# Layer 3's attention of three images among the last expert tiles, in a four-layer hybrid network

## The chip, the cores and the metric

The kernel runs on one core of a Trainium2 chip, as one launch. The metric is the device time in microseconds, the median of several runs of the whole program; one further execution is recorded by the hardware profiler, and all views below come from that one.

The engines are named as the profile names them: PE is TensorE's matmul, PEld its weight load, DVE is VectorE, ACT is ScalarE, POOL is GpSimd, SP is SyncE. An engine works through its own instructions in order, and semaphores make it wait for others. A name with q behind it (ACTq, SPq, POOLq) is the engine issuing DMAs.

## What is computed

Input `x` is (4, 256, 32, 32): four images (B) of 1024 tokens (L) with 256 channels (D), so 4096 tokens (T). Everything is float32. Four layers follow one another:

- Layer 0: a Mamba-2 block with squeeze-and-excitation. Layer 1: a non-local block of 1x1 convolutions. Neither is touched.
- Layer 2: self-attention, then a mixture of experts. Every token goes to the best two of eight experts (E); an expert is two matrices, 256x1024 and 1024x256, with an exact gelu between.
- Layer 3: a linear attention with batch norm, and then an LSTM of 1024 steps over the tokens.

Cut to what matters here:

```python
# layer 2, feed forward: _ln_t normalises each token over its channels
logits = xf @ Wg + bg
top_w, top_i = top_k(logits, 2); top_w = softmax(top_w)
out = sum over e of  w_dense[:, e] * (gelu(xf @ W1[e] + b1[e]) @ W2[e] + b2[e])
t = t + out
# layer 3, attention, for each image; f = _ln_t(t)
query, key = f @ W_qk[0] + b_qk[0], f @ W_qk[1] + b_qk[1]
sm = softmax(key, axis=tokens)
lam = einsum('bnd,bne->bde', sm, f @ W_v + b_v)
bn = batchnorm(lam)            # over the images and the value channels
t = t + einsum('bnd,bde->bne', query, bn)
# layer 3, feed forward: an LSTM over the tokens, h and c start at 0
i, f, o = sigmoid(x_t U + b + h V);  g = tanh(x_t U_c + b_c + h V_c)
c = h * c + i * g;  h = o * tanh(c)
```

The batch norm of `lam` runs over all four images, so nothing behind it can start before the last image's `lam`. The first three images' `lam` do not need the last image.

## The kernel before

**Experts** (`_layer2_experts`). Tokens are scattered by expert into a DRAM buffer `sorted`, and worked in tiles of 256 rows (TS). There are 36 tiles (NTILE), in an order written out at the head of the function: 17 "first" tiles (NFULL), filled from the routing of images 0 to 2 alone, so that they run while the last image's routing is still worked out beside them (`last_image`, advanced by `next(parts, None)`); then 16 "more" tiles (NMORE), with 3 half tiles of 128 rows (NHALF) spread between them. Three further halves (NREST) stand behind a runtime condition, `tc.If(need > NHALF)`; with this input they are not run, but every engine passes there.

For each tile, `fetched` (two tiles ahead) has POOL gather the expert's weights `w` (128 x 4360 floats, L1249) and the token rows (L1255). `turned` computes where each result goes (`place`, DVE, L1271 or L1273), transposes the rows on PE (`pt`, L1277) and copies them to `uT` (DVE, L1279). `worked` runs the first matrix on PE (`ph`, L1300), gelu on ACT (`hT`, L1292), the second matrix for the two halves of the tile (`po`, L1334), adds the bias and scales on DVE (`y`, L1339 and L1340), and scatters to a DRAM buffer `results` (POOL, L1341). A half tile goes through `raw` instead (L1314 to L1322). `turned` of the next tile is called between the two `po` of a tile; the instruction scheduler then decides each engine's order. `po` has two PSUM banks in the pool `moe_ps2`, `ph` three, `pt` one. A scatter of one tile and the next one are kept in order by `place`, which is written while the scatter before it may still read its other buffer.

**Layer 3's attention** (`_layer3_attention`) starts when the last expert result has landed. Image by image: SP loads the two results of each token (`y_in`, L1486, sixteen loads of 512 KB, three buffers of two); DVE adds them to the rows (L1491) and takes the statistics (L1495, L1496), and a short Newton iteration (`_rsqrt`) gives the scale; ACT normalises (`rows`, L1476); PE transposes (`p_x`, L1442) and DVE copies to `u` (L1446); PE multiplies by the key matrix (L1517), ACT adds the bias (L1522), DVE takes the maximum (L1529), ACT the exponential with its sum (L1532); PE transposes the keys (`p_k`, L1542), DVE copies (`kt`, L1544), PE accumulates `p_u` (L1546); a last product with the value matrix gives `lam` (L1556, L1560). The rows are also transposed to `x_l` (ACT copies, L1445). The queries (L1573) and the batch norm (`bn_stats` L668, L1592) follow the last image.

**The LSTM** (`_layer3_lstm`): a lead-in (folding the queries' matrix into `lam`, L1642, the first norm, L1707 to L1748, and the input products, L1674), and then 1024 steps in which PE, DVE and ACT answer one another. Its weights `b_l`, `w_u`, `w_v` and the four matrices of `w_l3` are loaded on ACT's queue (L1404, L186) as the attention begins.

The order in which the code writes its work out is all that the programmer sets; each engine's final order comes from a list scheduler which goes by modelled costs. Two lines are kept for the tile order:

```python
order.append(("more", i))
order += [("half", h) for h in range(i * NHALF // NMORE, (i + 1) * NHALF // NMORE)]
```

Of the kernel before, what the change touches and what calls it, by code (L numbers as in the profile page):

```python
# [11 lines left out]
F32 = mybir.dt.float32  # L12
# [7 lines left out]
P = 128  # L20
# [32 lines left out]
NTILE = NFULL + NMORE + NHALF  # L53
ROW = D + 2
# [29 lines left out]
def _setup(s):  # L84
# [33 lines left out]

    s.spread = s.const.tile([NBLK, NBLK, P], F32, name="spread")
    nc.vector.tensor_copy(s.spread, _bc(s.ident[:NBLK, :NBLK], 2, P))  # L120
# [69 lines left out]
def _layernorm(s, u):  # L190

    nc = s.nc
    with ExitStack() as ctx:
        pool = ctx.enter_context(s.tc.tile_pool(name="ln", bufs=2))
        ps = ctx.enter_context(s.tc.tile_pool(name="ln_ps", bufs=2, space=PSUM))
        ps1 = ctx.enter_context(s.tc.tile_pool(name="ln_ps1", bufs=1, space=PSUM))
        var = ps1.tile([NBLK, W], F32, name="var")
# [20 lines left out]
        for i in range(NBLK):  # L218
            t = bass.ts(i, W)
            wide = ps.tile([P, W], F32, name="wide")  # L220
            nc.tensor.matmul(wide, s.spread[:, i, :], rstd, start=True, stop=True)
            nc.vector.tensor_mul(u[:, :, t], u[:, :, t], _bc(wide, 1, C))
# [496 lines left out]

def _layer2(s):  # L720

# [3 lines left out]
    with ExitStack() as ctx:  # L725
        m = SimpleNamespace(
            keep=ctx.enter_context(tc.tile_pool(name="moe_keep", bufs=1)),
            one=ctx.enter_context(tc.tile_pool(name="moe_one", bufs=1)),
            pool=ctx.enter_context(tc.tile_pool(name="moe_head", bufs=2)),
# [23 lines left out]
        m.views = dram_disjoint_views(s.sorted, 2 * NT)  # L753
        m.counts = None
        _layer2_attention(s, m)
        _layer2_experts(s, m)


def _layer2_attention(s, m):
    nc, tc = s.nc, s.tc  # L760
    scale = D**-0.5
    with ExitStack() as ctx:
        keep = ctx.enter_context(tc.tile_pool(name="l2_keep", bufs=1))
        u = keep.tile([P, C, T], F32, name="u")
# [98 lines left out]
def _head(s, m, b, psum):  # L863
# [97 lines left out]
    before = m.counts  # L961
# [81 lines left out]
def _table(s, m, name, n, tiles):  # L1043
# [5 lines left out]
    t = lambda shape, x: m.one.tile(shape, F32, name=f"{name}_{x}")  # L1049
# [15 lines left out]
def _pick(s, m, name, mine, values):  # L1065

    nc = s.nc
    n, K = mine.shape[1:]
    w = m.one.tile([P, n, K], F32, name=f"{name}_w")
    nc.vector.tensor_mul(w, mine, _bc(values, 1, n))  # L1070
    of = m.one.tile([P, n], F32, name=f"{name}_of")
    nc.vector.tensor_reduce(of, w, AX.X, ALU.add)
    return of


def _weight_rows(s, m, name, expert):

    nc = s.nc
    n = expert.shape[1]
    row = m.one.tile([P, n], F32, name=f"{name}_row")  # L1080
    nc.vector.tensor_scalar(row, expert, float(E - 1), float(P), ALU.min, ALU.mult)
    rows = m.keep.tile([P, n], U32, name=f"{name}_rows")
    nc.vector.tensor_scalar_add(rows, row, s.token[:, :1])
    return rows


def _count(s, m, name, values, n, size, least):

    nc = s.nc
    edges = m.one.tile([P, n], F32, name=f"{name}_edges")  # L1090
    nc.vector.tensor_scalar(edges, m.marks[:, :n], float(size), float(least), ALU.mult, ALU.add)
    over = m.one.tile([P, E, n], F32, name=f"{name}_over")
    nc.vector.tensor_tensor(over, _bc(values, 2, n), _bc(edges, 1, E), ALU.is_ge)
    held = m.one.tile([P, E], F32, name=f"{name}_count")
# [4 lines left out]
def _taken(s, m, name, n, first, tiles):  # L1099

    nc = s.nc
    taken = m.one.tile(list(tiles.shape), F32, name=f"{name}_taken")
# [5 lines left out]
def _first_tiles(s, m):  # L1108
# [7 lines left out]
    base = m.one.tile([P, E], F32, name="f_base")  # L1116
# [11 lines left out]
def _part_tiles(s, m, name, n, A, tiles, start, ahead):  # L1128
# [9 lines left out]
    if K > E:  # L1138
        over = m.one.tile([P, n], F32, name=f"{name}_over")
        nc.vector.tensor_scalar(over, of, float(E), -float(E), ALU.is_ge, ALU.mult)  # L1140
        nc.vector.tensor_add(of, of, over)
# [3 lines left out]
    base = m.one.tile([P, K], F32, name=f"{name}_base")  # L1145
# [4 lines left out]
    at = m.one.tile([P, n, A], F32, name=f"{name}_at")  # L1150
    nc.vector.tensor_tensor(at, _bc(own, 2, A), _bc(s.token[:, :A], 1, n), ALU.add)
    counts = m.one.tile([P, K], F32, name=f"{name}_counts")
# [4 lines left out]
    valid = m.one.tile([P, n, A], F32, name=f"{name}_valid")  # L1157
# [15 lines left out]
    places = m.one.tile([P, n * A], F32, name=f"{name}_ahead")  # L1173
# [8 lines left out]
def _other_tiles(s, m):  # L1182
# [5 lines left out]
    tiles = m.one.tile([P, 2 * E], F32, name="m_tiles")  # L1188
    start = m.one.tile([P, 2 * E], F32, name="m_start")
    nc.vector.tensor_sub(tiles[:, :E], most, m.taken)  # L1190
    nc.vector.tensor_scalar_mul(start[:, :E], m.taken, float(TS))
    yield
    nc.vector.tensor_scalar_mul(start[:, E:], most, float(TS))
    nc.vector.tensor_tensor(tiles[:, E:], m.counts, start[:, E:], ALU.is_gt)
# [3 lines left out]
    begin = m.one.tile([P, E], F32, name="h_start")  # L1198
    nc.vector.tensor_add(begin, taken[:, :E], taken[:, E:])
# [3 lines left out]
    left = m.one.tile([P, E], F32, name="h_left")  # L1203
# [3 lines left out]
    total = m.one.tile([P, 1], F32, name="h_total")  # L1207
# [7 lines left out]
def _layer2_experts(s, m):  # L1215

    nc, tc = s.nc, s.tc
    results = iter(dram_disjoint_views(s.results, 2 * (NFULL + NMORE) + NHALF + NREST))  # L1220
    order = [("first", i) for i in range(NFULL)]
    for i in range(NMORE):
        order.append(("more", i))
        order += [("half", h) for h in range(i * NHALF // NMORE, (i + 1) * NHALF // NMORE)]
    with ExitStack() as body:
        wp = body.enter_context(tc.tile_pool(name="moe_w", bufs=2))
        hp = body.enter_context(tc.tile_pool(name="moe_h", bufs=2))
        rp = body.enter_context(tc.tile_pool(name="moe_r", bufs=3))
        ps = body.enter_context(tc.tile_pool(name="moe_ps", bufs=3, space=PSUM))
        ps2 = body.enter_context(tc.tile_pool(name="moe_ps2", bufs=2, space=PSUM))  # L1230

        def psum():
            return ps2.tile([P, W], F32, name="p_head")

        def last_image():
            yield from _head(s, m, B - 1, psum)
# [3 lines left out]

        def fetched(j):

            kind, i = order[j]
            if kind != "first":
                for _ in parts:
                    pass
            rows, slots = m.tiles[kind][:2]
            w = (wp if j % 3 else m.w).tile([P, NEXP], F32, name="w")
            nc.gpsimd.indirect_dma_start(  # L1249
                w, None, s.d["w12"], bass.IndirectOffsetOnAxis(rows[:, i : i + 1], 0)  # L1250
            )
            A = slots.shape[2]
            row = m.row.tile([P, 2, ROW], F32, name="row")
            for a in range(A):
                got = nc.gpsimd.indirect_dma_start(  # L1255
                    row[:, a, :], None, s.sorted,
                    bass.IndirectOffsetOnAxis(slots[:, i, a : a + 1], 0),
                )
                if kind == "first":

                    m.full.append(got)
            return w, row[:, :A]

        def turned(j):

            kind, i = order[j]
            row = held[j][1]
            A = row.shape[1]
            place = rp.tile([P, 2], U32, name="place")[:, :A]
            if kind == "first":  # L1270
                nc.vector.tensor_copy(place, row[:, :, D + 1])  # L1271
            else:
                nc.vector.tensor_add(place, row[:, :, D + 1], m.tiles[kind][2][:, i, :])  # L1273
            pt = ps2.tile([P, C, A, P], F32, name="pt", bufs=1)
            for k in range(C):
                for a in range(A):
                    nc.tensor.transpose(pt[:, k, a, :], row[:, a, bass.ts(k, P)], s.ident)  # L1277
            uT = rp.tile([P, C, TS], F32, name="uT")[:, :, : A * P]
            nc.vector.tensor_copy(uT, pt.rearrange("p k a t -> p k (a t)"))  # L1279
            return place, uT  # L1280

        def worked(w, row, place, uT, lead):

            A = row.shape[1]
            w1 = w[:, : C * HID].rearrange("p (k n) -> p k n", k=C)
            w2 = w[:, C * HID : C * HID + NHC * D].rearrange("p (k n) -> p k n", k=NHC)
            b1 = w[:, C * HID + NHC * D :][:, :NHC]
            b2 = w[:, C * HID + NHC * D + NHC :]
            hT = hp.tile([P, NHC, TS], F32, name="hT")

            def gelu(n, ph):
                nc.scalar.activation(  # L1292
                    hT[:, n, : A * P], ph, AF.Gelu, bias=b1[:, n : n + 1]
                )

            if A == 2:
                for n in range(NHC):
                    ph = ps.tile([P, W], F32, name="ph")[:, :TS]
                    for k in range(C):
                        nc.tensor.matmul(  # L1300
                            ph, w1[:, k, bass.ts(n, P)], uT[:, k, :],
                            start=k == 0, stop=k == C - 1,
                        )
                    gelu(n, ph)
                    if n % 2:
                        next(parts, None)
                        next(parts, None)
            else:

                raw = rp.tile([P, HID], F32, name="raw", bufs=2)  # L1310
                for i in range(HID // W):
                    ph = ps.tile([P, W], F32, name="ph")
                    for k in range(C):
                        nc.tensor.matmul(  # L1314
                            ph, uT[:, k, :], w1[:, k, bass.ts(i, W)],
                            start=k == 0, stop=k == C - 1,
                        )
                    nc.vector.tensor_copy(raw[:, bass.ts(i, W)], ph)
                for i in range(HID // W):
                    ph = ps.tile([P, W], F32, name="ph")  # L1320
# [664 lines left out]
```

## Time and profile before

| | |
|---|---|
| median of 3 runs | 3393.04 us (3390.83 to 3394.68) |
| profiled execution, its own time | 3408.06 us |
| its span | 3406.3 us |
| mean granted TensorE clock | 0.973 |
| busy: PE / DVE / ACT / POOL | 3177.1 / 1997.0 / 1233.9 / 378.8 us |
| chain that ended last: PE / DVE / ACT / issue / DMA / POOL | 72 / 14 / 5 / 3 / 2 / 1 % |

By stages of the span, PE's busy time and clock:

| stage | window, us | PE busy, us | clock |
|---|---|---|---|
| layers 0 and 1 and layer 2's attention | 0 to 780 | 675.1 | 0.92 to 0.95 |
| first expert tiles, the last image's routing beside | 780 to 1040 | 240.0 of 260 | 0.96 |
| more expert tiles | 1040 to 1255 | 215.0 of 215 | 1.00 |
| the last expert tiles | 1255 to 1311 | 51.4 of 56 | 1.00 |
| layer 3's attention | 1311 to 1450 | 107.8 of 139 | 0.86 |
| lead-in of the LSTM | 1450 to 1475 | 23.9 of 25 | 0.93 |
| LSTM | 1475 to 3406 | 1863.9 of 1931 | 1.00 |

The windows are cut by hand from the trace. A matmul record of the profile is one pass of PE: a float32 product of this kernel shows two records, a transpose one. "Clock" is the share of full speed that was granted to PE in the window.

### The profile page before, as it was taken

How to read it: one execution, taken by the hardware profiler on the slowest of the kernel's cores; microseconds unless marked ns; L12 is line 12 of the kernel's file. 1: busy time of each engine (PE TensorE's matmuls, PEld its weight loads, DVE VectorE, ACT ScalarE, POOL GpSimd, SP SyncE). 2: the span in 40 equal slices, each digit the busy share in tenths (PEclk: the TensorE clock that was granted, in tenths of full speed). 3: DMA queues.
4: the chain of work that ended last, by engine and by line, in shares of the span. 5: the costliest groups of instructions: out<-in, count | busy, mean ns of one | idle time of the engine just before them, and what ended most of it. 6: DMA issues, size and time to landing. Idle time of an engine off the chain costs nothing.

```text
span 3406.3 us, 146430 instructions
## 1 busy us (share of the span) xinstructions
PE 3177.1 (93%) x65186; PEld 2489.1 (73%) x65186; DVE 1997.0 (59%) x8389; ACT 1233.9 (36%) x5057; POOL 378.8 (11%) x468
## 2 busy tenths in 40 slices
PE   7788899998899996999999999999999999999888
PEld 4465344446788884688888888888888888888776
DVE  5696534452211115557777777776777767776666
ACT  4633222223222222433434334343343343443333
POOL 0083002223433330000000000000000000000000
PEclk9899899999999997999999999999999999999999
DMA  1291001115555654000000000000000000000000
GB/s 69 67 298 34 10 0 38 38 36 203 187 195 206 230 212 148 0 3 5 4 11 4 5 11 4 11 4 4 11 4 5 10 4 5 10 5 4 10 4 10
DMA packets 78058, 180.50 MB, mean 53 GB/s; under 512 B 6256, under 2 KB 63920, under 8 KB 72816
## 3 DMA queue, kind: packets, MB, share of 16 engines
q0 software_dynamic: 14880, 106.99, 8.5%
q1 hardware_dynamic: 60624, 59.12, 5.9%
q8 instruction: 511, 8.37, 1.0%
q10 hardware_dynamic: 1920, 5.00, 0.4%
q14 instruction: 123, 1.01, 0.1%
HBM read 111.26 MB, written 59.84 MB: 50 GB/s over the span
## 4 chain that ended last, share of the span: by engine, by line
PE 72%; DVE 14%; ACT 5%; issue 3%; DMA 2%; POOL 1%; ACTq 0%; DVEq 0%; POOLq 0%
PE p_c L1826 11%; PE p_c L1817 8%; PE ph L1300 6%; PE po L1334 6%; DVE turned L1867 6%; PE p_i L1817 5%; PE p_o L1826 5%; PE p_i L1826 5%; PE p_o L1817 5%; PE beside L1767 4%; PE p_mm L850 3%; PE p_s L814 2%; ACT a_o L1868 2%; DVE x L1880 2%; ACT th L1878 1%
## 5 line engine op out<-in xcount | busy, mean ns | idle before, releaser
L1868 ACT ACTIVATE add<-turned 128x8 f32<-128x8 f32 x1024 | 214.3, 209 | 1011.4 <-DVE turned L1867 1011.4
L1826 PE MATMUL p_c<-w_v,x 128*4 128x64 f32 x16368 | 416.7, 219 | 60.6 <-DVE x L1880 57.9
L1817 PE MATMUL p_c<-xg,shift 128*128 128x64 f32 x2048 | 446.0, 299 | 0.0
L1826 PE MATMUL p_o<-w_v,x 128*4 128x64 f32 x16368 | 417.8, 219 | 0.0
L1826 PE MATMUL p_i<-w_v,x 128*4 128x64 f32 x16368 | 417.4, 219 | 0.0
L1817 PE MATMUL p_i<-xg,shift 128*128 128x64 f32 x2048 | 407.7, 281 | 0.0
L1867 DVE STREAM_TRANSPOSE turned<-p_c 128x64 f32<-128x64 f32 x1024 | 255.7, 250 | 253.9 <-PE p_c L1826 220.0
L1817 PE MATMUL p_o<-xg,shift 128*128 128x64 f32 x2048 | 396.4, 275 | 0.0
L1817 PEld LDWEIGHTS p_c<-xg,shift 128*128 128x128 f32 x2048 | 304.9, 188 | 117.6 <-DVE turned L1867 0.4
L1826 PEld LDWEIGHTS p_c<-w_v,x 128*4 128x4 f32 x16368 | 227.9, 85 | 180.8 <-DVE x L1880 102.0
L1880 DVE TENSOR_TENSOR x<-a_o,th 128x8 f32<-128x8 f32 x1024 | 171.2, 167 | 246.0 <-ACT th L1878 246.0
L1817 PEld LDWEIGHTS p_o<-xg,shift 128*128 128x128 f32 x2048 | 311.4, 192 | 0.0
L1817 PEld LDWEIGHTS p_i<-xg,shift 128*128 128x128 f32 x2048 | 305.1, 188 | 0.0
L1826 PEld LDWEIGHTS p_o<-w_v,x 128*4 128x4 f32 x16368 | 281.9, 87 | 0.8 <-issue 0.5
L1826 PEld LDWEIGHTS p_i<-w_v,x 128*4 128x4 f32 x16368 | 281.6, 87 | 0.3
L1867 DVE STREAM_TRANSPOSE turned<-p_i 128x64 f32<-128x64 f32 x1024 | 271.9, 266 | 0.9 <-PE p_i L1826 0.7
L1292 ACT ACTIVATE hT<-ph,w 128x256 f32<-128x256 f32 (+1 forms) x288 | 131.3, 465 | 355.8 <-PE ph L1300 267.3
L1300 PE MATMUL ph<-uT,w 128*128 128x256 f32 x1056 | 241.6, 386 | 19.6 <-DVE uT L1279 11.3
L1867 DVE STREAM_TRANSPOSE turned<-p_o 128x64 f32<-128x64 f32 x1024 | 255.6, 250 | 0.9 <-PE p_o L1826 0.3
L1334 PE MATMUL po<-w,hT 128*128 128x256 f32 x1104 | 251.1, 380 | 2.7 <-ACT hT L1292 1.5
L1868 ACT ACTIVATE a_o<-turned 128x8 f32<-128x8 f32 x1024 | 213.3, 208 | 95.4 <-DVE cell L1871 4.5
L1300 PEld LDWEIGHTS ph<-uT,w 128*128 128x128 f32 x1056 | 203.2, 194 | 50.2 <-DVE uT L1279 12.1
(499 smaller groups left out, 4395.0 us busy)
## 6 DMA issues: line engine op xcount, KB each, us to landing
sorted<-zeros SPq DMA_DIRECT2D x32, 1032.0 KB
y_in<-results SPq DMA_DIRECT2D x16, 512.0 KB
x<-in_x_dram SPq DMA_DIRECT2D x8, 512.0 KB
tokens<-rows SPq DMA_DIRECT2D x4, 1024.0 KB
x<-tokens SPq DMA_DIRECT2D x8, 512.0 KB
out_dram<-x_l SPq DMA_DIRECT2D x64, 64.0 KB
results<-y,place POOLq DMA_INDIRECT x69
w_l<-in_w_l_dram ACTq DMA_DIRECT2D x1, 1092.0 KB
```

What stands on the lines that cost most here:

```text
L814: nc.tensor.matmul(p_s[:, h, :], q[:, k, q0 : q0 + P], u[:, k, b * L + h * W : b * L + (h + 1) * W], start=k == 0, stop=k == C - 1,)
L850: nc.tensor.matmul(p, v[:, n, bass.ts(c, P)], prT[:, n, :], start=n == 0, stop=n == TPI - 1,)
L1292: nc.scalar.activation(hT[:, n, : A * P], ph, AF.Gelu, bias=b1[:, n : n + 1])
L1300: nc.tensor.matmul(ph, w1[:, k, bass.ts(n, P)], uT[:, k, :], start=k == 0, stop=k == C - 1,)
L1334: nc.tensor.matmul(po, hT[:, n, bass.ts(a, P)], w2[:, n, :], start=n == 0, stop=n == NHC - 1,)
L1767: nc.tensor.matmul(p[bass.ts(i, R), :], rows[:, k, bass.ts(g, R)], w_u[:, k, at : at + GQ // GC], start=k == 0, stop=k == C - 1, tile_posi ...
L1817: nc.tensor.matmul(p[:, :H], shift[:, row * B : row * B + P], xg[n][:, g, bass.ts(i, H)], start=True, stop=t == 0,)
L1826: nc.tensor.matmul(p[R * i : R * i + B, :H], hs[:, t - 1, bass.ts(k, B)], w_v[:, k, i * GQ + g * H : i * GQ + (g + 1) * H], start=False, s ...
L1867: nc.vector.transpose(zt.rearrange("p c w -> p (c w)"), pz[g][:, :H])
L1868: nc.scalar.activation(dst.rearrange("p (c b) -> p c b", c=C), zt[:, :, :B], f)
L1878: nc.scalar.activation(th, cell[:, :, 1], AF.Tanh)
L1880: nc.vector.tensor_mul(h, a_o, th)
```

## The change

- A new tile order. The 17 first tiles, then 14 "more" tiles; then the last five, half, more, half, more, half. The tables are built so that these last five tiles (from tile NLAST = 31 on) hold tokens of the last image only: "more" tiles now come in two kinds, those up to an expert's last row of images 0 to 2 and those after. `_other_tiles` has more operations on its small tables for that.
- So the results of images 0 to 2 have all been scattered when tile 30 ends. `first_images()` is a generator of layer 3's work: image 0's rows to `u`; image 0's keys to `lam` in turn with image 1's rows to `u`; image 1's keys in turn with image 2's rows. It is advanced two steps at each place `beside(n)` of the tiles 31 to 35, and emptied before the `If`.
- Behind the `If`, `_layer3_last_image` does the last image's rows in turn with image 2's keys and the first three images' transposes to `x_l`; then the last image's keys, the queries and the batch norm.
- `y_in` loads are single (512 KB) with two buffers; a load is issued after the add two before it.
- The expert stage is two functions, `_first_experts` (17 tiles) and `_last_experts` (19), with pools of their own; at the change of pools the buffers' last users are waited for. In the second one `po` has one PSUM bank, `pt` takes turns with layer 3's transposes and products in two banks; `hT` has one buffer, `place` and `uT` two. Two more banks are layer 3's `p_u`.
- `u`, `lam` and `q` live in a new pool over both layers; `spread` goes from the constants to the norm that uses it; `x` by channel is written over the input's copy, and the LSTM's hidden states have a tile of their own. The LSTM's weights (`b_l`, `w_u`, `w_v`, `wq`) are loaded, on ACT's queue still, where `_layer3_lstm` begins.

The core of the diff:

```diff
+        m.order = [("first", i) for i in range(NFULL)]
+        m.order += [("more", i) for i in range(NLAST - NFULL)]
+        for i in range(NHALF):
+            m.order.append(("half", i))
+            if NLAST - NFULL + i < NMORE:
+                m.order.append(("more", NLAST - NFULL + i))
...
+def _last_experts(s, m):
...
+        l3 = SimpleNamespace(
+            pool=ctx.enter_context(tc.tile_pool(name="l3", bufs=2)),
+            y=ctx.enter_context(tc.tile_pool(name="l3_y", bufs=2)),
+            ps=ctx.enter_context(tc.tile_pool(name="l3_ps", bufs=2, space=PSUM)),
+            pu=ctx.enter_context(tc.tile_pool(name="l3_pu", bufs=1, space=PSUM)),
...
+        def first_images():
+            yield from _rows_to_u(s, l3, 0)
+            for b in range(B - 2):
+                yield from _in_turn(_keys(s, l3, b, nc.vector), _rows_to_u(s, l3, b + 1))
...
+            m.rp = body.enter_context(tc.tile_pool(name="moe_r", bufs=2))
+            m.ps = body.enter_context(tc.tile_pool(name="moe_ps", bufs=3, space=PSUM))
+            m.po = body.enter_context(tc.tile_pool(name="moe_po", bufs=1, space=PSUM))
+            m.hT = m.rp.tile([P, NHC, TS], F32, name="hT", bufs=1)
+            m.bank = lambda name: l3.bank()
...
+                def beside(n):
+                    if j >= NLAST:
+                        for _ in range(2):
+                            next(parts, None)
...
+                done = _worked(s, m, j, *ahead.pop(), lead, beside)
...
+            for _ in parts:
+                pass
...
+            with tc.If(need > NHALF):
...
+        _layer3_last_image(s, l3)
...
+def _rows_to_u(s, l3, b, split=False):
...
+    load()
+    load()
+    yield
+    for i, (g, k) in enumerate(todo):
+        xr = s.xr[:, bass.ts(b * G + g, TPB), :]
+        nc.vector.tensor_add(xr, xr, ys[i])
+        if len(ys) < len(todo):
+            load()
+        yield
...
+        first = chain(_keys(s, l3, last - 1, nc.scalar), *(by_channel(b) for b in range(last)))
+        for _ in _in_turn(_rows_to_u(s, l3, last, split=True), first):
+            pass
+        for _ in _in_turn(_keys(s, l3, last, nc.vector), by_channel(last)):
+            pass
+        for _ in queries():
+            pass
...
+        bias, fold, mask, shift = _lstm_constants(s, keep)
+        w_u = _weights(s, keep, "w_u")
+        w_v = _weights(s, keep, "w_v")
+        wq = keep.tile([P, C, D], F32, name="wq")
+        nc.scalar.dma_start(wq, s.d["w_l3"][:, :D].rearrange("(k p) n -> p k n", p=P))
```

## The prediction

> **What bounds the kernel now.** I read the windows view first, over the end of the expert stage and the attention of layer 3 (columns: window, its length, busy us and instruction count of each engine, granted TensorE clock, DMA share, GB/s):
>
> ```profile
> 1242.00:1256.00 14.00, 14.00 (x69) 12.32 (x68) 1.88 (x7) 3.79 (x8) 4.87 (x5) 1.00 0.57 208
> 1311.00:1326.00 15.00, 1.28 (x6) 0.87 (x6) 9.41 (x32) 1.93 (x4) 0.00 (x0) 0.52 0.88 309
> 1326.00:1347.00 21.00, 15.97 (x38) 6.76 (x36) 15.40 (x36) 7.36 (x13) 0.00 (x0) 0.69 0.58 184
> 1347.00:1380.00 33.00, 27.30 (x103) 17.86 (x104) 28.63 (x97) 10.91 (x21) 0.00 (x0) 0.84 0.25 80
> 1410.00:1446.00 36.00, 32.84 (x145) 22.67 (x144) 13.97 (x31) 8.42 (x14) 0.00 (x0) 1.00 0.00 0
> ```
>
> The experts are bound by PE: 14.00 of 14 us. Then PE does almost nothing for 15 us while layer 3 loads the expert results, and for 54 us more it is busy, but at a granted clock of 0.69 and 0.84. The chain of waits shows a full expert tile on its own, and the hand-over (start, us, what):
>
> ```profile
> 1241.58 6.91 PE ph L1300 x32
> 1248.49 3.45 PE po L1334 x16
> 1251.94 0.44 PE pt L1277 x4
> 1252.38 3.46 PE po L1334 x16
> 1255.84 6.91 PE ph L1300 x32
> ...
> 1282.53 28.61 DMA results<-y,place
> 1311.85 3.32 DMA b_l<-in_b_l_dram
> 1315.19 10.98 DMA y_in<-results
> 1326.26 1.24 DVE x L1491
> ```
>
> A full tile is 6.91 + 3.45 + 0.44 + 3.46 = 14.26 us of PE without a gap, starting at 1241.58 here; the half tile before it ran from 1218.9 to 1227.3, about 8.3. The last `po` ends at 1306.7, the first layer-3 load is issued at 1311.9. Last, VectorE's own timeline, for what stands in its queue around a `po`:
>
> ```profile
> 1252.10 0.16 DVE L1273 TENSOR_TENSOR place<-row,more_added 128x2 uint32<-128x2 f32 x1 [9.66 <-DMA results<-y,place]
> 1252.17 0.42 DVE L1339 TENSOR_TENSOR y<-po,w 128x256 f32<-128x256 f32 x1
> 1252.51 0.68 DVE L1279 COPY uT<-pt 128x512 f32<-128x512 f32 x1
> ```
>
> The add that empties the first `po` bank came 1.5 us after that `po` was full (1248.49 + 3.45 = 1251.94, add done 1252.59), because it stands behind `place`, which waits for the scatter before it. Today a second bank hides this. The LSTM, 1473 to the end at 3406.3, is 57% of the span; its steps are not touched, so I price it at nothing, unless the new addresses of its tiles matter, which no row shows.
>
> **The segment that gains.** I compare from the start of the last five tiles (three halves, two full: 3 × 8.3 + 2 × 14.25 = 53.4 us of PE) to the point where the lead-in of the LSTM begins (1449.6). Before, that is 53.4 + (1449.6 − 1306.7) = 196 us.
>
> After, the PE work put before the runtime `If` is: the tiles, 53.4; images 0 and 1 in full. One image is 16 transposes at 0.11 (`pt` x4 takes 0.44) = 1.8; the keys, 7.0 (L1517 x16 took 7.03 at 1420.32); 16 `p_k` transposes, 1.8; 32 `p_u` matmuls at 0.216, 6.9; 8 for the values, 1.8: 19.3 us, so 38.6 for two, and 1.8 for image 2's transposes. Together 40.4.
>
> The gaps. The loads of `y_in` are 512 KB each, sixteen of them; the new pool has 2 buffers, so a load waits for the add two before it. In the quiet hand-over of before, issue to add took 4.5 us (1311.91 to 1316.41) and an add 1.2. The first load cannot start before tile 30's last scatter, which lands about 11 us after tile 31's start (`place` of the tiles shown starts 10.5 to 12.4 after the tile). VectorE runs in order, and image 0's adds stand ahead of the `y` adds of tile 32, whose single `po` bank then holds PE: I walk this to about 4 us (0 to 10). PE's next work in its order is the transposes of image 0, a block between tiles 32 and 33; they need eight loads in pairs, 4 × (4.5 + 1.2) = 23 us, statistics and the 2.6 us of Newton steps, after a start at about 11 + 5: ready near 42, while tile 32 ends near 27 + what waits beside it. I take 10 (3 to 16). For the ping-pong PE–VectorE–PE of `p_k`, `kt`, `p_u`, the row of 1410 to 1446 gives 9% idle: 4 us on 40 (2 to 12, as ScalarE's alternation of gelu and exp adds table loads; one took 1.28 before).
>
> `If` is therefore passed at 53.4 + 40.4 + 4 + 10 + 4 = 112. After it only image 3 is late: from load to its keys 25 us (before, 1311.9 to 1336.7 for the first image, beside 2.6 MB of weights; image 2's 17.5 us of keys and values and the other images' channel transposes lie under it), from the keys to the lead-in 29.3 (1420.32 to 1449.6): 54 (50 to 60). The LSTM's weights are moved from 1311 to behind the queries on ScalarE's queue: `wq`, last, has 1.8 MB to wait for, about 5 us at the 350 GB/s of the first window plus the latency, 8 us from an issue at the last query (1448.75 in before's times); its first user, L1642, ran at 1454.4. That is 2 us late (0 to 8). Sum 168, against 196: **−28** (150 to 200, so −46 to +4).
>
> **What it costs elsewhere.** *One `po` bank instead of two* in tiles 17 to 30. `place` starts on average 11.3 us after the tile (six tiles: 12.4, 11.3, 11.1, 11.6, 10.5, 11.2); the add is done 0.6 later, while PE wants the bank at 10.8. That is 1.2 us a tile (0.2 if the scatter is early, 2.3 at the latest of the six). In about a third of the tiles the new order sets the next tile's first `ph` pairs ahead and most of it is covered. 9.3 × 1.2 + 4.7 × 0.3 = **+12** (3 to 32).
>
> *The pools change hands at tile 17*: PE's first `ph` waits for every scatter of tile 16, then `place` and `uT`. Before, the nearest such stop is the end of the experts, 1306.7 to 1311.7; with `place` and `uT` 5 to 6; **+5** (0 to 10: the next weights are fetched across it).
>
> *A cold PE.* Gaps of over 3 us at tile 17 and in tile 32 leave a lowered clock: the first image's 8 key matmuls took 6.45 us where 3.44 is the full rate, so 3 us a gap at most; **+2** (0 to 9). The Trainium skill ("TensorE: Matmul & The Clock Gate", section "The HAM clock gate") says half the clock holds until about 3.4 us of sustained work, 1.7 us lost for each long gap. That speaks against a change that puts waits among dense tiles; with it the term would be about 5 for the three gaps ahead of the `If` and the time 3 us more. The trace is worse than the rule: 69% and 84% over 54 us, (1 − 0.69) × 15.97 + (1 − 0.84) × 27.3 = 9.4 us lost, because the work there was broken.
>
> *The rest*: some 25 more small VectorE operations on the tables of the new tile order, 0.2 to 1 us each, lie beside PE-bound tiles (VectorE busy 1.88 of 14); price nothing, 10 us at most if the order were needed before it is ready. One buffer for `hT` and two for `place` cost nothing, as PE goes in order and the same scatter is waited for.
>
> Sum: −28 + 12 + 5 + 2 = **−9 us**. The profiled execution took 3408.06 (span 3406.3), 15.0 above the median of 3393.04; the difference carries over: 3399 profiled, **3384** median.
>
> One more rule: "DMA: Bandwidth & Descriptors", section "Queues, rings and completion order", has each DMA engine alternate packets between the queues with work. An expert's 2.23 MB fetch and a `y_in` load would then halve each other. Quiet rows cannot show that; by it a load beside a fetch would take about 1.5 us longer, 6 us for image 0, and the sum would be −3.
>
> **Rivals.** *Nearly all hidden.* Half the time the DMA engines idle in the expert stage (shares 0.49 to 0.59), and rows could be ready when tile 32 ends. Then the two gaps shrink from 14 to 4, the `po` term to 3, the hand-over to 2: −9 − 10 − 9 − 3 = −31, **3362**. Against it: VectorE's order fixes the adds ahead of `y`.
>
> *Slower: VectorE's queue.* Every `y` add, `place` and `uT` of tiles 32 to 35 stands behind adds that wait for loads in pairs. My walk takes 5.7 us a round. Image 0 has four rounds, image 1 some two that PE feels. Each us more of latency costs 6 us; from about 2.7 us more (7.2 us a load, beside the fetches) it is over 0.2% slower than before. A fetch took 7 to 9 us of full DMA; a load that waits behind one takes 10: +33 − 9 = +24, **3417**.
>
> *It does not do what it says.* In the code, 84 places beside the last tiles are offered for about 106 steps, and image 0 forms a block between tiles rather than lying beside them. If the ping-pong costs 14 instead of 4, the gain goes: **3394**.
>
> **Chances.** Forecast 0.38, hidden 0.24, VectorE's queue 0.26, no gain 0.12. A difference of 0.2%, 6.8 us, is about what a measurement of this kernel can tell from none. Of the forecast, 0.26 lies beyond it as faster, 0.10 within, 0.02 slower; the hidden case is all faster, VectorE's all slower; of the last, 0.02, 0.06, 0.04. So 0.52, 0.16, 0.32. The forecast's own range is 3368 to 3396; for 8 in 10 it reaches from a little beyond the hidden case, 3352, to VectorE's, 3415.
>
> **What would show it.** In the changed profile: `po` of tiles 17 to 30 waits for the `y` add about 1.2 us each; a PE gap of 5 us at tile 17; two gaps around tile 32, 4 and 10 us, released by image 0's loads; 54 us from the `If` to the lead-in; granted clock near 1 from there on. A tile pace of 14.25 refutes the `po` term, gaps above 25 us bring the slower rival, and a longer LSTM would be something I have not priced.

## The result, and the profile after

The changed kernel takes 3425.8 us (median of 4 runs, 3421.0 to 3433.8), the kernel before 3393.9 beside it: a ratio of 1.0097, 95% interval 1.0073 to 1.0121, or 25 to 41 us slower. The forecast was 3384, its range 3352 to 3415. The runs below were made on several chips, on which the kernel before takes 3394 to 3409; so each is given as a ratio to the kernel before on its own chip.

The profiled execution of the changed kernel has a span of 3419.4 us, 13.1 more than before. First the waits between the start of tile 17 and that of tile 31 (engine, line, waited for: us in all, times, longest):

```profile
DVE place L1301 <- DMA results<-y,place: 147.9, 14, 12.9
PE po L1363 <- DVE y L1369: 24.0, 13, 3.4
```

Before, PE had no wait at `po` in these tiles. Now it waits 13 times for the add that empties the bank, 24.0 us in all. PE's timeline for tile 30 shows it (start, us, engine, line, operation; in brackets the idle time before it and what ended it):

```profile
1264.44 3.72 PE L1363 MATMUL po<-w,hT 128*128 128x256 f32 x16 [0.80 <-DVE y L1369]
1268.00 6.21 PE L1331 MATMUL ph<-uT,w 128*128 128x256 f32 x28
1274.05 3.62 PE L1363 MATMUL po<-w,hT 128*128 128x256 f32 x16
1277.50 0.71 PE L1305 MATMUL bank<-ident,row 128*128 128x128 f32 x5
1279.56 3.72 PE L1363 MATMUL po<-w,hT 128*128 128x256 f32 x16 [1.35 <-DVE y L1369]
...
1298.35 3.62 PE L1363 MATMUL po<-w,hT 128*128 128x256 f32 x16
1311.10 5.29 PE L1363 MATMUL po<-w,hT 128*128 128x256 f32 x16 [9.13 <-DVE y L1369]
1325.77 2.12 PE L1574 MATMUL bank<-ident,rows 128*128 128x128 f32 x8 [9.38 <-issue]
1332.33 1.94 PE L1574 MATMUL bank<-ident,rows 128*128 128x128 f32 x8 [4.45 <-DVE u L1578]
1334.64 8.88 PE L1617 MATMUL bank<-u,w_kv 128*128 128x512 f32 x16 [0.37 <-DVE u L1578]
```

(1264.44 is the second `po` of tile 29; in the two lines of 1274.05 and 1279.56 tile 30's own two `po` stand, with the wait between them.) VectorE and POOL beside the wait of 1.35 us:

```profile
1279.01 0.16 DVE L1301 TENSOR_TENSOR place<-row,half_added 128x1 uint32<-128x1 f32 x1 [9.99 <-DMA results<-y,place]
1279.09 0.42 DVE L1369 TENSOR_TENSOR y<-po,w 128x256 f32<-128x256 f32 x1
```

```profile
1269.41 0.97 POOL L1276 DMA_INDIRECT w<-in_w_dram,more_rows  x1 [1.89 <-issue]
1270.68 0.99 POOL L1371 DMA_INDIRECT results<-y,place  x1 [0.30 <-issue]
```

This is a ring. The second `po` of tile 29 ends at 1268.1; that frees its weights, and POOL fetches the next 2.23 MB at 1269.4; the scatter of tile 29 is queued behind that, at 1270.7, and has landed at 1279.0; only then does `place` run, and behind it the add; only then is the bank free for the second `po` of tile 30.

The later lines of PE's timeline are tile 32. Its second `po` waits 9.13 us, image 0's transposes 9.38 and 4.45 more, and the work behind each gap is slow: 5.29 us for 16 records of `po` against 3.62, 8.88 for 16 key records against 7.03. VectorE's timeline has the cause of the first:

```profile
1304.13 1.23 DVE L1588 TENSOR_TENSOR x<-x,y_in 128x1024 f32<-128x1024 f32 x1 [8.66 <-DMA y_in<-results]
...
1309.41 1.23 DVE L1588 TENSOR_TENSOR x<-x,y_in 128x1024 f32<-128x1024 f32 x1 [0.66 <-DMA y_in<-results]
1310.56 0.15 DVE L1301 TENSOR_TENSOR place<-row,half_added 128x1 uint32<-128x1 f32 x1
1310.62 0.42 DVE L1369 TENSOR_TENSOR y<-po,w 128x256 f32<-128x256 f32 x1
```

Three of image 0's adds and their statistics stand ahead of the `y` add, and the first load, issued at 1295.9, was added at 1304.1, 8.2 us later, where before it took 4.5. The windows that answer to those of before (tile 31 and the first matrix of tile 32; on to image 0's keys; up to the `If`; up to the lead-in):

```profile
1283.00:1298.00 15.00, 14.76 (x66) 11.35 (x65) 3.69 (x8) 5.26 (x15) 6.81 (x7) 1.00 0.75 270
1298.00:1345.00 47.00, 23.16 (x71) 14.29 (x70) 32.64 (x101) 9.23 (x17) 3.51 (x3) 0.71 0.61 211
1345.00:1408.00 63.00, 62.31 (x293) 47.28 (x291) 27.00 (x66) 26.83 (x55) 3.88 (x4) 1.00 0.07 23
1408.00:1468.00 60.00, 53.35 (x236) 36.12 (x236) 32.22 (x102) 28.75 (x55) 0.00 (x0) 0.94 0.12 35
```

PE is busy 62.31 of 63 us once image 0's rows are there. The idle and cold stretch of before has not gone: part of it, 23.16 us busy in 47 at a clock of 0.71, now lies in front.

By stages of the profiled executions (us; the tile starts are the first `ph` of a tile, "14 full tiles" is tiles 17 to 30 after and 14 times 14.25 before, the next column is the remaining five tiles and the attention):

| kernel | tile 0 to tile 17 | 14 full tiles | to the lead-in | lead-in to the first LSTM step | sum |
|---|---|---|---|---|---|
| before | 270.4 | 199.5 | 196.0 | 25.2 | 691.1 |
| before, second profile | 271.0 | 199.5 | 196.4 | 23.6 | 690.5 |
| after | 275.0 | 233.3 | 184.7 | 25.5 | 718.5 |

So 27 to 28 us are lost here: +4 to 5, +33.8, −11.3, 0 to +2. The spans differ by only 13.1 because in this execution the first expert tile began 8.9 us earlier (774.8 against 783.8) and the LSTM was 5.4 us shorter (1926.0 against 1931.4 from the first step's tanh to the end). Both vary between executions: the first tile began at 778.7 to 783.8 in the four profiles of the kernel before and its variants, and at 773.1 to 780.4 in the ten of the changed kernel and its variants; and 2.9 us of the 5.4 are three slow first steps of the LSTM (2.33, 3.25 and 2.94 us instead of 1.87) in the profile before, which the profile after has not. No run isolates the rest.

### The profile page after: what moved, and what is told of

It is laid out like the page before. It is cut to its first block, busy times and chain, and to the rows that moved or that the text cites. A ratio compares the mean times of both kernels' runs of the same rounds, so it can differ in the third digit from the quotient of the medians.

```text
span 3419.4 us, 146684 instructions
## 1 busy us (share of the span) xinstructions
PE 3173.5 (93%) x65186; PEld 2489.8 (73%) x65186; DVE 1994.8 (58%) x8394; ACT 1240.8 (36%) x5069; POOL 379.7 (11%) x468
## 4 chain that ended last, share of the span: by engine, by line
PE 45%; DVE 8%; ACT 4%; issue 1%; ACTq 0%; DVEq 0%
PE p_c L1992 11%; PE p_c L1983 8%; DVE turned L2033 6%; PE p_i L1983 5%; PE p_i L1992 5%; PE p_o L1992 5%; PE p_o L1983 5%; PE beside L1933 4%; ACT a_o L2034 2%; DVE hs L2046 2%; ACT th L2044 1%; PE beside L1840 1%; PE beside L1873 1%; PE p_u L1651 0%; PE var L1883 0%
## 5 line engine op out<-in xcount | busy, mean ns | idle before, releaser
L1992 PE MATMUL p_c<-w_v,hs 128*4 128x64 f32 x16368 | 416.2, 219 | 60.2 <-DVE hs L2046 57.6
L1992 PE MATMUL p_o<-w_v,hs 128*4 128x64 f32 x16368 | 416.2, 219 | 0.0
L1992 PE MATMUL p_i<-w_v,hs 128*4 128x64 f32 x16368 | 416.1, 219 | 0.0
L1992 PEld LDWEIGHTS p_c<-w_v,hs 128*4 128x4 f32 x16368 | 227.3, 85 | 180.7 <-DVE hs L2046 101.7
L2046 DVE TENSOR_TENSOR hs<-a_o,th 128x8 f32<-128x8 f32 x1024 | 170.8, 167 | 245.7 <-ACT th L2044 245.7
L1363 PE MATMUL po<-w,hT 128*128 128x256 f32 x1104 | 259.7, 389 | 33.1 <-DVE y L1369 33.1
L1992 PEld LDWEIGHTS p_o<-w_v,hs 128*4 128x4 f32 x16368 | 281.1, 87 | 0.0
L1992 PEld LDWEIGHTS p_i<-w_v,hs 128*4 128x4 f32 x16368 | 281.0, 87 | 0.0
L1363 PEld LDWEIGHTS po<-w,hT 128*128 128x128 f32 x1104 | 212.8, 195 | 67.1 <-DVE y L1369 37.1
## 6 DMA issues: line engine op xcount, KB each, us to landing
sorted<-zeros SPq DMA_DIRECT2D x32, 1032.0 KB, 15.4
```

What stands on the lines that cost most here:

```text
L1363: nc.tensor.matmul(po, m.hT[:, n, bass.ts(a, P)], w2[:, n, :], start=n == 0, stop=n == NHC - 1)
L1992: nc.tensor.matmul(p[R * i : R * i + B, :H], hs[:, t - 1, bass.ts(k, B)], w_v[:, k, i * GQ + g * H : i * GQ + (g + 1) * H], start=False, s ...
L2046: nc.vector.tensor_mul(h, a_o, th)
```

## The experiments

**Theory:** the loss is the single `po` bank, emptied late by VectorE's order, and the gain at the end is halved because image 0's rows come late to a PE that stands waiting for them. **Rivals:** the tiles wait for something else and PE only shows the last wait; or the loss lies behind tile 31.

**A second profile of the kernel before.**

> The kernel before, unchanged, for a second profile. If the 15 us by which its first profiled execution stood above the median of its runs are an accident of that execution, this one lies near 3393 and shows where the accident was (the first stages, where the changed kernel's first tile began 8.9 us earlier in its profile, and the first LSTM steps). If the profiler itself costs 15 us, it lies near 3408 again, and the two profiles are to be compared as they are.

3408.8 us, ratio 1.0002 (0.9993 to 1.0012) on a chip where its runs lie at 3404 to 3414. Its profiled execution took 3403.5: the profiler does not cost 15 us. The first profiled execution, 3408.06, lies within the runs of this chip and outside its own timed runs (3390.8 to 3395.8); it may have run on another chip, which the record does not say. In the prediction the 15.0 us cancel: 3384 is 3393 − 9 with or without them. The sum of its stages above, 690.5 against 691.1, shows that these are steady.

**Two banks for `po`.**

```diff
-            m.ps = ...tile_pool(name="moe_ps", bufs=3, space=PSUM)
-            m.po = ...tile_pool(name="moe_po", bufs=1, space=PSUM)
+            m.ps = ...tile_pool(name="moe_ps", bufs=2, space=PSUM)
+            m.po = ...tile_pool(name="moe_po", bufs=2, space=PSUM)
```

> The changed kernel with two PSUM banks for po and two for ph instead of one and three. Theory (the single po bank is emptied late, since its add stands behind place on VectorE): the tiles 17 to 30 go back to 14.25 us each, 33.8 us are won there, and the whole is at about 3392, level with the kernel before. First rival (these tiles wait for something else, weights or the row gathers, and PE only shows the last wait): the gaps stay, with another releaser, and the time stays within 8 us of 3426. Second rival (the loss is in the last five tiles and behind): tiles 17 to 30 get faster, but the time does not follow.

Ratio 1.0001 (0.9987 to 1.0015): level with before, as the theory has it. The 14 tiles take 204.3 us, most of them 14.3. The first rival falls, and so does the second, since the time followed the tiles. One `ph` bank had to be given up for it. The end does not profit: PE no longer waits at tile 32's `po`, but stands 26.1 us in front of image 0's transposes instead (to the lead-in 187.3 us).

```profile
1272.81 7.07 PE L1363 MATMUL po<-w,hT 128*128 128x256 f32 x32
1305.98 2.12 PE L1574 MATMUL bank<-ident,rows 128*128 128x128 f32 x8 [26.10 <-issue]
```

**The scatter ahead of the fetch.** The weight fetch is ordered behind the last scatter issued:

```diff
+    if j > NFULL + 1:
+        _after(s, got, m.put, "scatter first")   # order on POOL, no wait added
```

> The changed kernel, with each expert weight fetch of tiles 19 on put behind the last scatter of the tile before it on POOL's queue, no other edit. Theory (place waits 11 us into a tile because the scatter is queued behind the 2.23 MB fetch): the scatter lands some 4 us after the tile's start, place no longer holds the add, and tiles 17 to 30 win about 30 us though po keeps one bank; the first load of image 0 starts about 6 us earlier as well: 3386 to 3392. Rival (the row gathers, or the fetch now 1.3 us later, become the wait): under 10 us.

Ratio 0.9989 (0.9974 to 1.0004); the 14 tiles take 200.6 us with one bank still. On POOL the scatter now goes first, and `place`, which followed it by 8.3 us above, follows by 2.5:

```profile
1249.28 0.98 POOL L1382 DMA_INDIRECT results<-y,place  x1 [1.29 <-PE ph L1342]
1250.56 0.98 POOL L1285 DMA_INDIRECT w<-in_w_dram,more_rows  x1 [0.30 <-ACT hT L1336]
```

```profile
1251.78 0.16 DVE L1312 TENSOR_TENSOR place<-row,half_added 128x1 uint32<-128x1 f32 x1 [2.78 <-DMA results<-y,place]
```

Image 0's first load is issued at 1268.8, 3.6 us behind a fetch issued at 1265.2, and its add follows 9.6 us later. It starts 10.5 us after tile 31's start instead of 12.8, not 6 us earlier as expected. To the lead-in it takes 185.0 us, 184.7 after the change: PE now waits 15.4 us at tile 32's `po`.

**The order on VectorE alone.**

```diff
-        nc.vector.tensor_add(place, row[:, :, D + 1], ...)
+        put = nc.vector.tensor_add(place, row[:, :, D + 1], ...)
+        if j > NFULL:
+            _after(s, put, m.added, "the bank first")   # m.added: the y add
```

> The changed kernel, one po bank and the scatter behind the fetch as changed, but with place held behind the add that empties the bank in tiles 18 to 30: an order on VectorE, no buffer more. Theory: PE then waits only for the add itself, 0.2 us a tile, and tiles 17 to 30 come to 200 to 206 us instead of 233; the whole at a ratio to before of 0.999 to 1.003. Rival (one bank is too few whatever the order): 225 us or more.

Ratio 1.0003 (0.9990 to 1.0015), and 203.1 us for the 14 tiles. No buffer was added and the scatter lands as late as before, but now the add comes first:

```profile
1224.84 0.42 DVE L1380 TENSOR_TENSOR y<-po,w 128x256 f32<-128x256 f32 x1 [8.68 <-PE po L1374]
1226.04 0.16 DVE L1310 TENSOR_TENSOR place<-row,more_added 128x2 uint32<-128x2 f32 x1 [0.78 <-DMA results<-y,place]
```

(The scatter that this `place` waits for was issued at 1217.8, 8.2 us before it.) One bank is enough for a pace of 14.5 us. The end is no better here either: 188.8 us to the lead-in. Each of the three mendings breaks the ring at another link, and each brings back about 30 us of the 33.8.

**One bank in the kernel before.**

```diff
-                po = ps2.tile([P, D], F32, name="po")
+                po = ps2.tile([P, D], F32, name="po", bufs=1)
```

> The kernel before with one PSUM bank for po instead of two, in all its 36 tiles, nothing else. Theory: PE waits for the add behind place here too, 1 to 3 us a tile and more where the pause lowers the clock: 30 to 70 us slower than before, ratio 1.009 to 1.020. Rival (the stall in the changed kernel comes from its two buffers for place and uT, not from the bank): under 8 us slower.

Ratio 1.0156 (1.0139 to 1.0173), 53 us on 3395: the part alone does the harm, without the new order, layout or buffers for `place` and `uT`. The group of all `po` in the profile before, and then here (busy us, mean ns of one, idle us before them and what ended it):

```profile
L1334 PE MATMUL po<-w,hT 128*128 128x256 f32 x1104 | 251.1, 380 | 2.7 <-ACT hT L1292 1.5
```

```profile
L1334 PE MATMUL po<-w,hT 128*128 128x256 f32 x1104 | 265.3, 396 | 50.5 <-DVE y L1339 50.4
```

The wait is for the same add, 50.4 us in all, and the `po` themselves take 14 us longer, as behind the gaps above.

**Nothing of layer 3 beside the tiles.** `beside` does nothing, and the generator is emptied behind tile 35.

> The changed kernel with nothing of layer 3 beside the last five tiles: its three images are worked out between tile 35 and the runtime If, pools and tile order as changed. If the laying-between itself wins about 11 us, as the segment from tile 31 to the lead-in says (184.7 us against 196), this is slower by that or more, since only one image is overlapped less: 3435 to 3460. If the new waits at tile 32 eat all that is laid beside, it is the same or faster: 3415 to 3430.

Ratio 1.0068 (1.0053 to 1.0083), somewhat faster than the change itself, if anything (the intervals touch). The end takes 183.4 us against 184.7. So as the change was made, laying PE's work between the tiles won nothing over leaving it behind; the 11 us are there without it. The likely source is the order of the tiles, which lets loads, adds and statistics begin before the last tile (the first load is issued at 1295.0 here, 12.7 us after tile 31's start); no run takes that away alone. The wait at tile 32's `po` is here too, 7.3 us, so this run does not show what laying between is worth without it.

**Both mendings.** Scatter first and two banks together:

> Changed kernel with both mendings, the scatter ahead of the weight fetch and two po banks. Theory (what is left of the loss is PE's wait for image 0's rows in front of tile 33, whose loads share the DMA engines with two weight fetches): tiles 17 to 30 at 14.3 us, but a gap of some 20 us in front of image 0's transposes, where scatter_first showed 15.4 at the po of tile 32 and 2.7 behind it, and two_po 26.1 at the transposes; the time within 6 us of scatter_first, ratio to before 0.997 to 1.000. Rival (the bank held by VectorE's adds is what counts in tile 32 too): the gap goes with the bank, 12 us or more below scatter_first.

Ratio 0.9978 (0.9968 to 0.9988). To the lead-in it takes 178.1 us, and a gap of 14.2 us is left before image 0's transposes. The expectation named the gap and the time, within 6 us of `scatter_first`; the two ratios cannot be told apart. In the profiles the end is 6.9 us shorter than in `scatter_first` (178.1 against 185.0), so a part of the rival may be true: the bank counts at tile 32 as well.

**Layer 3 begun two tiles later.**

```diff
-                    if j >= NLAST:
+                    if j >= NLAST + 2:
```

> As sf_two, with layer 3's steps beside tiles 33 to 35 only instead of 31 to 35, so that image 0's transposes stand in PE's order inside tile 34, 20 us later, and image 1's keys behind tile 35. Theory (the transposes stand too early in PE's order for rows that arrive about 37 us after tile 31's start): the gap of some 20 us closes, no other opens, 12 to 18 us below sf_two, ratio to before 0.993 to 0.996. Rival (the work is only moved, and what PE gains at tile 33 it pays in softmax waits behind tile 35): within 5 us of sf_two.

Ratio 0.9999 (0.9987 to 1.0010): no gain, where 0.993 to 0.996 was expected. The gap is still there, at another place:

```profile
1282.66 6.77 PE L1353 MATMUL ph<-w,uT 128*128 128x512 f32 x8 [11.45 <-DVE uT L1320]
```

Tile 33 waits for its `uT`, and that copy, at 1282.2, stands on VectorE behind adds of image 0 that wait for loads:

```profile
1262.31 1.23 DVE L1599 TENSOR_TENSOR x<-x,y_in 128x1024 f32<-128x1024 f32 x1 [8.69 <-DMA y_in<-results]
...
1279.86 1.23 DVE L1599 TENSOR_TENSOR x<-x,y_in 128x1024 f32<-128x1024 f32 x1 [5.08 <-DMA y_in<-results]
```

The program's order had moved, but the scheduler still set the adds early. To the lead-in it takes 181.6 us.

**The same without laying between.** `sf_two` with an empty `beside`:

> As sf_two, with nothing of layer 3 offered beside the tiles; loads, adds and statistics of image 0 still come as early as their data. Without the gap at tile 33 but with every softmax of images 0 and 1 open behind tile 35 (about 5 us of PE idle each): by the theory between sf_two and sf_two_late; ratio to before 0.995 to 0.999. If it equals sf_two_late, laying PE's work between tiles is worth nothing, and the gain lies in the loads, adds and statistics alone.

Ratio 1.0032 (1.0019 to 1.0045), slower than both, where it was expected between them. To the lead-in it takes 192.9 us. It has the 12.5 us gap at tile 33 too, so it does not measure what laying between is worth without that gap.

**The adds held behind tile 33's copy.**

```diff
-        nc.vector.tensor_add(xr, xr, ys[i])
+        put = nc.vector.tensor_add(xr, xr, ys[i])
+        if b == 0:
+            _after(s, put, l3.hold, "the tile first")   # the copy of tile 33's uT
```

> As sf_two_late, with image 0's adds held on VectorE behind the copy of tile 33's uT. Theory (sf_two_late lost its gain because that copy stood behind adds that wait for loads: an 11.5 us gap at tile 33): that gap goes, image 0's rows come some 8 us later but still fall beside tile 34; 6 to 12 us below sf_two_late and below sf_two, ratio to before 0.994 to 0.997. Rival (the later rows move the gap to tile 34 or behind tile 35): within 4 us of sf_two_late.

Ratio 0.9949 (0.9933 to 0.9965): 12 to 23 us faster than the kernel before, the fastest here. To the lead-in 175.8 us. Tile 33's copy now comes at 1272.1, before image 0's first add:

```profile
1272.05 0.41 DVE L1320 COPY uT<-bank 128x256 f32<-128x256 f32 x1
```

Tiles 31 to 33 run without a gap, and one of 9.6 us is left, in tile 34:

```profile
1275.19 3.60 PE L1353 MATMUL ph<-w,uT 128*128 128x512 f32 x8
...
1302.91 0.66 PE L1589 MATMUL bank<-ident,rows 128*128 128x128 f32 x2 [9.60 <-issue]
```

From the first tile to the LSTM's first step its profile takes 676.7 us, `sf_two_late`'s 684.4: 8 us, within the 6 to 12 expected, of the 17 by which the two ratios differ. The ratios come from two chips, with 4 to 5 us on either side each; no run separates what is left.

**Three buffers for `y_in`.**

```diff
-            y=...tile_pool(name="l3_y", bufs=2)
+            y=...tile_pool(name="l3_y", bufs=3)
...
-        y = m.rp.tile([P, D], F32, name="y", bufs=3)
+        y = m.rp.tile([P, D], F32, name="y", bufs=2)
```

> As hold, with three buffers for y_in and three loads ahead instead of two (and two for y instead of three, for the room). Theory (rows are paced by rounds of load and add, two in flight): another 2 to 6 us below hold. Rival (by then all is paced by the DMA engines or hidden): within 2 us of hold.

Ratio 0.9968 (0.9958 to 0.9978). The end of the profile has what was expected, 171.8 us to the lead-in and a gap of 4.0 instead of 9.6, but the runs are not faster than those of `hold` (the intervals touch). The profiles do not contradict that: from the first tile to the LSTM's first step they take 675.6 and 676.7 us, because `hold`'s came to tile 17 in 272.1 us and this one's in 275.1. Whether that difference is chance or comes with the third buffer, no run shows.

**The scatter order in the kernel before.** The same edit as in `scatter_first`:

> The kernel before with each weight fetch of tiles 19 on put behind the last scatter of the tile before it, nothing else: does that mending win anything without the new layout? Theory: no, since the kernel before hides the late place behind its second po bank; PE keeps 14.25 us a tile and the time stays within 4 us, ratio 0.999 to 1.001. Rival (part of hold's gain is the scatter order alone, through an earlier hand-over behind the last tile): 5 us or more faster.

Ratio 1.0006 (0.9997 to 1.0015): nothing. What `hold` wins is not the scatter order by itself, but the layout with its new waits taken out.

## Why the prediction was wrong, step by step

The direction was wrong, by the size of two terms, the `po` term and the end; the clock, which the prediction priced apart, has a share in both.

- **The `po` term (+12, bounds 3 to 32; measured +33.8): the step that failed most.** The mechanism was right, and its three mendings show it; the size was not. 6.6 of the 33.8 us are the clock, next point. The other 27 are nearly all the ring: the second `po` (3.6), the fetch and the scatter behind it until `place` (12.0 on average) and the add (0.6), 16.2 us against 14.25, thirteen times over, 25 us. The prediction's sum is the same ring with 11.3 us in place of 12.0, and its 11.3 came from six late tiles. Over the sixteen full tiles before from 1039.9 to 1284 it is 11.8: the old trace had most of the difference, and the sample missed it. The relief for a third of the tiles does not exist: a `ph` that PE does earlier does not shorten the ring, and the three tiles of the timeline in which it stands directly ahead of the waiting `po` still wait 0.8, 1.9 and 2.9 us.
- **The cold PE (+2, bounds 0 to 9).** In tiles 17 to 30 four gaps of 1.9 to 3.5 us were followed by a `po` of 5.2 to 5.4 us in place of 3.72, 1.5 to 1.7 us each, 6.6 in all; the granted clock falls to 0.50 or 0.51 inside each of these `po`. Three other gaps, of 2.1, 2.3 and 2.9 us, were followed by a `po` of 3.72 us, so the length of the gap does not settle it. The page of the Trainium skill that the prediction weighed ("TensorE: Matmul & The Clock Gate", section "The HAM clock gate") has full clock after about 3.4 us of sustained work; half a clock until then would lose 1.7 us, an estimate from that figure, and the four losses are about that size. What the prediction had not was the gaps. Two more losses came at tile 32, 1.7 and 1.9 us.
- **The end (−28; measured −11.3).** The gaps at tile 32 were put at 4 and 10; they were 9.1 and 13.8, and with the cold clock behind them 26 us. The step that failed is the load: 4.5 us from the quiet hand-over of before, 8.2 beside the weight fetches, 3.7 more for the first pair. The prediction's estimate from the Trainium skill, "DMA: Bandwidth & Descriptors", section "Queues, rings and completion order", was 1.5 us more a load beside a fetch. From issue to landing, four loads that ran beside a fetch took 7.5 to 9.2 us and the other twelve 3.8 to 5.3; that the fetches slow them is argued from these times, since no run moves the loads away from the fetches. The first load came at 12.8 us after tile 31's start, not 11. From the `If` to the lead-in it took 60 us, at the upper bound given (50 to 60): 28 until the last image's keys instead of 25, and 32 from there instead of 29.3; why, no run shows.
- **The change of pools (+5; measured +4.3)** and **the late LSTM weights (+2; lead-in 25.5 against 23.6 and 25.2)** fit, and so does the price of nothing on the tables in the first stage: tiles 0 to 16 keep their time to 0.3 us.
- **The rival on VectorE's queue (3417)** named the end's mechanism, and `sf_two_late` and `hold` show it: 11.5 us at tile 33 that go when the adds are held. But it was priced for the tiles from 32 on, and the greater part of the loss lies before; that its 3417 stands near the measured 3426 is luck.
- **The rival that the change does not do what it says** holds in part: with nothing offered beside the tiles the kernel is no slower (`not_beside`). It was priced as a wash of 3394 only because the `po` term was thought small.
- **Two slips that change little.** The add before was done 0.65 us after its `po` was full (1252.59 − 1251.94), not 1.5; the `po` term does not use the 1.5. And the fullest window that the prediction shows reads 309 GB/s, not 350, with which the wait for 1.8 MB of weights would be 5.8 us instead of 5.

## What to carry to other kernels

When a buffer is taken away, write down the ring that the buffer closes, add up its links over all rounds of the old trace and not over a few, and compare the sum with the pace; here 16.2 against 14.25 us. Then add what the clock loses behind the gaps that the ring opens. Such a ring can be opened where it is cheapest, and an order on one engine (the add before the address, the scatter before the fetch) did as much as a second bank. Work that is moved beside other work needs its inputs there first; look at what its own small instructions stand in front of on the other engines, and what its loads run beside.

## What the runs showed of the hardware

A scatter queued 1.3 us behind a 2.23 MB indirect fetch on POOL's queue reached `place` 8.3 us after its issue, and 2.5 us with the fetch behind it. And a busy PE can stay at a low clock: in the execution of `y_first` the windows of the first LSTM steps read

```profile
1470.00:1476.00 6.00, 5.63 (x121) 4.73 (x121) 2.79 (x14) 1.52 (x10) 0.00 (x0) 0.50 0.01 3
1476.00:1482.00 6.00, 6.00 (x124) 5.31 (x123) 2.25 (x11) 1.15 (x8) 0.00 (x0) 0.50 0.01 3
1482.00:1488.00 6.00, 6.00 (x127) 5.41 (x126) 2.60 (x14) 1.28 (x9) 0.00 (x0) 0.58 0.01 3
1488.00:1494.00 6.00, 6.00 (x191) 5.13 (x191) 4.26 (x21) 2.52 (x14) 0.00 (x0) 1.00 0.01 3
```

a clock of 0.50 over 12 us with PE busy in all but 0.4 of them, and steps of 3.23 us instead of 1.88, until it rises at once. The rule of the Trainium skill's page "TensorE: Matmul & The Clock Gate", section "The HAM clock gate", full clock after some 3.4 us of sustained work, does not describe these windows; the measurement decides. The profiled executions of other kernels show none to six such slow first steps, up to 7 us in all.
